# Two pairs of first maxima moved into the second layer's end, and three PSUM places made slices of one tile

## The chip, the core and the metric

The kernel runs on one core of a Trainium2 chip. TensorE (PE) multiplies matrices into PSUM, VectorE (DVE) and ScalarE (ACT) read PSUM and work elementwise, GpSimd (POOL) works in SBUF, SyncE (SP) issues most DMAs. The engines run their own instruction streams and wait for each other on semaphores. The metric is the device time of one execution in microseconds, median of the runs shown; lower is better.

## The reference, cut to what matters

The input is eight images of 32 x 32 positions with 256 channels. Three blocks follow each other: a hybrid of a 3x3 convolution (192 channels) and attention with relative position logits (8 heads of 8 channels), then plain attention with one head of 128, then a mixture of two of eight feed-forward experts.

```python
# layer 0, on the group-normalised image
conv_out = lax.conv_general_dilated(x, conv_w, ..., padding='SAME') + conv_b
logits = jnp.einsum('bnid,bnjd->bnij', qf, kf) + rel_w + rel_h
weights = jax.nn.softmax(logits, axis=-1)
attn = jnp.einsum('bnij,bnjd->bnid', weights, vf)
x = x + concatenate([conv_out, attn @ attn_w + attn_b], axis=3)
# layer 1, on the layer-normalised tokens t
w = softmax(Q @ K.T / sqrt(U)); t = t + (w @ V) @ W_o + b_o + norm(t)
# then the experts, on norm(t), chosen for each image by a router
```

## The kernel before, in words

The program goes through the eight images one after the other and keeps PE's instruction stream in the order in which the code is written (`manual_schedule` for PE). The other engines' streams in this part are ordered by the framework's scheduler. The framework puts in the semaphore waits, from the tiles that each instruction reads and writes. The expert layer comes after all images, as a part of its own (from L1025).

**The first layer's attention** (`conv_layer_attention`, L681) works on four *units* of an image, each 4 of 8 heads and 512 of 1024 queries. In `Unit.score` (L574) two matmuls (K=24, 512 columns) write a 128 x 1024 tile `lg` of logits, and DVE takes its maxima into `my` (L591). Sixteen of these, in eight pairs, give a unit its maxima. `Unit.fold` (L600) turns them (`pmx`), adds the row term and sends the result `mb` by three DMAs into row 32 of the operand `F`. Then `Unit.weigh` (L615) recomputes logits transposed, now with K=32, into `st` (128 x 512, one PSUM bank), and ACT writes their exponentials to `PT` (L631). `Unit.gather` (L633) multiplies `PT` with the values into `po`.

The loop at L694 counts steps `s`. A step scores one pair for unit `s // 8` and weighs one block of 128 keys for the unit ten steps back (`lead = NT + LAG = 10`). So three stretches come out: ten steps that only score (the **lead**), 22 that score and weigh, and ten that only weigh. In a step that does both, PE's order is score, weigh head 1, weigh head 3, gather half, score, weigh head 0, weigh head 2, gather half. In the steps that only weigh, heads 1 and 3 share one wide `lg` tile. Beside them stand the transposes and statistics of the next image (`norm_steps`, L295).

**The convolution** (`conv_steps`, L501) is 72 products an image, twelve to a tile `pc` (L515). ACT copies a full tile into `m` (L524, two buffers) and POOL adds it into the image `T` in up to four additions (L527 to L538). `Conv.run(n)` emits n products. They are spread as fillers: `more` and `fill` emit 36 of the next image's while the second layer starts, two stand in the second layer's end, and 34 fall in the lead, three to a step. Their tile comes from `place[0]`, which is `po_tile` during the fill and `st_tile` in the lead.

**The fill** (`attention_layer`, L758, and `input_steps`, L385): PE alternates the next image's projections (`pk`, `pvv`), its relative position products (`prel`, `tpw`), convolution products and the transposes of the normalised tokens (`tpn`, L779). POOL adds the tokens `n` (two buffers) into `T` at L780 and the bias `bo` at L784.

**The second layer's attention** (also `attention_layer`): eight blocks of rows. `scores(i)` writes `lg1`, DVE takes the row maximum, ACT the exponential; `turn(i)` transposes it through two `st` tiles, one copied out by DVE (L856) and one by ACT (L858); `gather(ib)` sums with the values into `po`; `project(ib)` multiplies with `W_o` into an `st` tile, which DVE adds into `T` (L880). Afterwards POOL sums `acc` for the router (L915, L917) and stores the image to `Td` (L922); `token_mean` (L925) finishes that sum, at step 5 of the next image.

**PSUM** has eight banks: `ps_lg` two tiles of two banks, `ps_st` three tiles of one, `ps_po` one. Everything but `lg`, `po`, `prel`, `tpw` and `tpx` goes through `st_tile`.

```python
def st_tile(name):
    return ps_st.tile([P, 512], FP, tag="st", name=name)      # bufs=3
```

Of the kernel before, what the change touches and what calls it, by code (L numbers as in the profile page):

```python
# [10 lines left out]
FP = mybir.dt.float32  # L11
I32 = mybir.dt.int32
AF = mybir.ActivationFunctionType
ALU = mybir.AluOpType
# [3 lines left out]
P = 128  # L18
# [18 lines left out]
def kernel(  # L37
# [54 lines left out]
    with ExitStack() as ph:  # L92
# [3 lines left out]


        ps_lg = ph.enter_context(tc.tile_pool(name="ps_lg", bufs=2, space=PSUM))
        ps_st = ph.enter_context(tc.tile_pool(name="ps_st", bufs=3, space=PSUM))
        ps_po = ph.enter_context(tc.tile_pool(name="ps_po", bufs=1, space=PSUM))  # L100


# [14 lines left out]
        def po_tile(name):  # L117
            return ps_po.tile([P, 512], FP, tag="po", name=name)

        def st_tile(name):  # L120
            return ps_st.tile([P, 512], FP, tag="st", name=name)


        raws = []
# [260 lines left out]
        def input_steps(b, held):  # L385
# [3 lines left out]
            xn = held["xn"].rearrange("p k a c j x -> p k (a c j x)")  # L389
            kq = work.tile([P, S], FP, tag="kq", name="kq")  # L390

            pv = st_tile("pvv").rearrange("p (j c) -> p j c", c=DK)
            for q in range(2):
                pk = st_tile("pk")
                for kc in range(KC):
# [30 lines left out]
            for g in range(NG):  # L426
# [12 lines left out]
                vb.rearrange("p (h d) -> p h d", d=DH).unsqueeze(1).to_broadcast([P, NT, NH, DH]),  # L439
                ALU.add,  # L440
            )
            yield 0.43, 2


# [10 lines left out]
            for which in range(2):  # L455
                for half in range(2):
                    prs = lg_tile("prel")
                    for i in range(16):
                        a = half * 16 + i
                        for g in range(NG):  # L460
                            rows = slice(DK + 32 * g, DK + 32 * g + 32)
                            dst = prs[:, g, i * 32 : (i + 1) * 32]
                            if which == 0:
                                table, mov, m = half_w, kqv[rows, :, a], WW - 1 - a
                            else:
                                table, mov, m = half_h, kqv[rows, a, :], HH - 1 - a
                            for k in range(2):
                                nc.tensor.matmul(
                                    dst[64 * k : 64 * k + 64], lhsT=table(rows, m, k), rhs=mov, start=True, stop=True
                                )  # L470
                        if i == 7:
                            yield 1.4, 4 - (which == half == 0)
                    for g in range(NG):
                        if which == 0:
                            dst = rw[g].rearrange("p (x y) -> p y x", y=WW)[:, half * 16 : half * 16 + 16, :]
                            src = prs[:, g, :].rearrange("p (y x) -> p y x", x=HH)
                        else:
                            dst, src = rh[g][:, half * 512 : (half + 1) * 512], prs[:, g, :]
                        if g == 0:
                            nc.vector.tensor_copy(dst, src)  # L480
                        else:
                            nc.scalar.copy(dst, src)
                    if which == 0 and half == 1:
                        for g in range(NG):
                            nc.sync.dma_start(out=rwd[g], in_=rw[g])
                    yield 1.4, 4 - (which == half == 0)

            for t4 in range(2):
                tp = lg_tile("tpw").rearrange("p q (t g c) -> p (q t) g c", t=2, g=NG)
# [51 lines left out]
        class Unit:  # L541
# [29 lines left out]
                self.pts = {}  # L571
                self.po = None

            def score(self, n, rwq):  # L574

                i, hl = divmod(n, HG)
                if hl == 0:
                    self.my = work.tile([P, WW, HG], FP, tag="my", name="my", bufs=2)
                my = self.my
                lg = lg_tile("lg")  # L580
                for a in range(2):
                    r = 32 * ((hl + 2 * a) % HG)
                    nc.tensor.matmul(  # L583
                        lg[:, a, :],
                        lhsT=self.F[r : r + 24, a, 0, i * P : (i + 1) * P],
                        rhs=KM[self.g][r : r + 24, a].rearrange("p e k -> p (e k)"),
                        start=True,
                        stop=True,
                    )

                nc.vector.tensor_reduce(  # L591
                    my[:, :, hl], lg.rearrange("p a (y x) -> p y a x", y=WW), AX.XY, ALU.max
                )
                if hl == HG - 1:
                    nc.vector.tensor_tensor(
                        my, my, rwq[:, self.half * 4 + i, self.g].rearrange("p (y h) -> p y h", h=HG), ALU.add
                    )
                    nc.vector.tensor_reduce(self.mx[:, i, :], my.rearrange("p y h -> p h y"), AX.X, ALU.max)
# [78 lines left out]

        NU = 2 * NG
        LAG = 2

        def conv_layer_attention(b, units, kq, rh, rwd, rwq, conv, early, ahead, more):  # L681

# [1 line left out]

            at = work.tile([P, NT, DK], FP, tag="at", name="at")
            units.append(Unit(1, kq, rh, rwd))
            left = conv.left
            lead = NT + LAG  # L690
            first = left % (3 * lead)
            conv.run(first)
            left -= first
            for s in range(NU * NT + lead + 2):  # L694
                u, j = divmod(s, NT)
                w, k = divmod(s - lead, NT)
                g, l = divmod(s - lead - 1, NT)
                score, weigh, gather = u < NU, 0 <= w < NU, 0 <= g < NU


                if score:
                    units[u].score(2 * j, rwq)
                    if weigh:
                        units[w].weigh(k, (1,), st_tile)
                        units[w].weigh(k, (3,), st_tile)
                    if gather and l:
                        units[g].gather(l, (0, 1))
                    units[u].score(2 * j + 1, rwq)
                    if weigh:
                        units[w].weigh(k, (0,), st_tile)  # L710
                        units[w].weigh(k, (2,), st_tile)
                    if gather:
                        units[g].gather(l, (2, 3) if l else (0, 1, 2, 3))
                else:
                    if weigh:
                        units[w].weigh(k, (0,), st_tile)
                        units[w].weigh(k, (2,), st_tile)
                        units[w].weigh(k, (1, 3), lg_tile)
                    if gather:
                        units[g].gather(l, (0, 1, 2, 3))  # L720
# [3 lines left out]
                    units[g - 1].settle(at)  # L724
                if g == NU:
                    more(NT // 2, 0)
                if not weigh:
                    todo = -(-left // (lead - s))
                    conv.run(todo)
                    left -= todo  # L730
                if s == 5:
                    early()
                if s > NU * NT:
                    next(ahead, None)
                if s % NT == 0 and 0 < u <= NU:
                    units[u - 1].fold(u - 1)
                if s % NT == 0 and 0 < u < NU - 1:
                    units.append(Unit(u + 1, kq, rh, rwd))
# [16 lines left out]
            more(0, 4)  # L755


        def attention_layer(b, fill, conv):  # L758

# [6 lines left out]
            fill(4.5)  # L768
            nT = pt_tile("nT").rearrange("p (k s) -> p k s", k=KC)
            for q in range(2):  # L770
                tps = [st_tile("tpn").rearrange("p (j t) -> p j t", j=4) for _ in range(KC)]
                for j in range(4):
                    t = q * 4 + j
                    n = work.tile([P, C], FP, tag="n", name="n", bufs=2)
# [6 lines left out]
                    fill(0.7)  # L781
                for kc in range(KC):
                    nc.scalar.copy(nT[:, kc, q * 512 : (q + 1) * 512], tps[kc].rearrange("p j t -> p (j t)"))
            nc.gpsimd.tensor_tensor(T[b], T[b], bo.to_broadcast([P, NT, C]), ALU.add)  # L784
            fill(1000.0)
            conv.whole()

# [58 lines left out]
            def turn(i):  # L846
                if i % NIB == 0:
                    pts[i // NIB] = pt_tile("pt").rearrange("p (j q) -> p j q", j=NT)
                for c in range(2):
# [2 lines left out]
                        jc = c * 4 + j  # L852
                        nc.tensor.transpose(tp[:, j, :], prs[:, i % 4, jc * P : (jc + 1) * P], ident)
                    dst = pts[i // NIB][:, c * 4 : c * 4 + 4, (i % NIB) * P : (i % NIB + 1) * P]
                    if c == 0:
                        nc.vector.tensor_copy(dst, tp)  # L856
                    else:
                        nc.scalar.copy(dst, tp)  # L858

            def gather(ib):  # L860
                po = po_tile("po1")
                pt = pts.pop(ib)
                for jc in range(NT):
                    nc.tensor.matmul(  # L864
# [19 lines left out]
            for i in range(NT):  # L884
                scores(i)
                if i < 2:
                    values(i)
                ib, odd = divmod(i - 3, NIB)
                if ib >= 0 and not odd:
                    os = gather(ib)  # L890
# [1 line left out]
                    turn(i - 1)  # L892
                if ib >= 0 and not odd and i + 1 < NT:
                    project(ib, os)
            turn(NT - 1)
            project(NT // NIB - 2, os)
            os = gather(NT // NIB - 1)
            conv.place[0] = st_tile
            conv.run(2)
            project(NT // NIB - 1, os)  # L900

# [53 lines left out]
        with tc.manual_schedule(engines={mybir.EngineType.PE, mybir.EngineType.DVE}):  # L955
# [12 lines left out]
                    next(other, None)  # L968
            for _ in other:
                pass  # L970
        with tc.manual_schedule(engines={mybir.EngineType.PE}):
            conv = Conv(0)
            means = []
            for b in range(B):
                last = b + 1 == B
                if not last:
                    T[b + 1] = load_image(b + 1)

                def early():
                    if means:  # L980
                        token_mean(*means.pop())

                def ahead():

                    yield from norm_steps(b + 1, held)

                now, held = held, {}
                conv.place[0] = st_tile
                steps = iter(()) if last else input_steps(b + 1, held)

                following = Conv(b + 1)
# [1 line left out]
                def more(n, products):  # L993
# [11 lines left out]
                    early,  # L1005
                    iter(()) if last else ahead(),
                    more,
                )
                conv = following

# [6 lines left out]
                        us -= took  # L1017
                        conv.run(products)

                means.append((b, *attention_layer(b, fill, conv)))  # L1020
                del T[b]
            token_mean(*means.pop())

# [282 lines left out]
```

## Time and profile before

The median of three runs is 2404.95 us (2403.57 to 2409.04). The profiled execution took 2407.99 us, with a span of 2406.2 us from its first to its last instruction, so 1.8 us lie outside the span.

| stretch of the profiled execution | us from the span's start | length, us | PE busy | granted clock |
|---|---|---|---|---|
| lead of the fifth image | 998.7 to 1031.6 | 32.9 | 31.9 | 0.90 |
| steps that score and weigh | 1031.6 to 1109.4 | 77.8 | 77.6 | 1.00 |
| steps that only weigh | 1109.4 to 1144.3 | 34.9 | 32.7 | 1.00 |
| fill | 1144.3 to 1181.2 | 36.9 | 36.5 | 1.00 |
| q and k of the second layer | 1181.2 to 1188.1 | 6.9 | 6.9 | 1.00 |
| the rest of the second layer | 1188.1 to 1232.3 | 44.2 | 44.2 | 1.00 |

Images follow each other every 231 to 234 us; the mean granted clock of the whole span is 0.974. Times of a stage are read off the starts of the first matmuls of each kind. A busy PE in a row is not PE at its peak, since a matmul's record also holds time in which it waits in PE's pipeline behind the one before it. In a row of the profile, "PE" is the matmul and "PEld" its weight load; one fp32 matmul of the code is two of each. "<-" after an idle time names what ended it.

### The profile page before, as it was taken

Reading aid. Unit: us, or ns where it says so; the run is one execution under the profiler, and the core shown is the slowest. Engines: PE = TensorE matmul, PEld = TensorE weight load, DVE = VectorE, ACT = ScalarE, POOL = GpSimd, SP = SyncE. Lnnn points to the kernel's source line nnn. Section 1 sums busy time; section 2 is a strip of 40 time slices with the busy share of each in tenths; the row PEclk is TensorE's granted clock in tenths of the full one; section 3 lists DMA queues with packets and bytes.
Section 4 is the critical chain, followed back from the end, with each engine's and each line's share of the span. In section 5 each row is a group of like instructions: output and inputs, shape, how many; then the busy total and the mean of one; then the engine's idle time right before and its main releaser. Section 6 shows DMA issues by size and latency. Waiting matters only on the chain. (4 is left out here: it accounts for less than half of the span.)

```text
span 2406.2 us, 41836 instructions
## 1 busy us (share of the span) xinstructions
PE 2317.1 (96%) x17273; PEld 1308.3 (54%) x17273; DVE 1481.2 (62%) x2653; ACT 1022.7 (43%) x1709; POOL 475.7 (20%) x446
## 2 busy tenths in 40 slices
PE   6999999999999999999999999999998789999998
PEld 5535743664366437633763376337533556666665
DVE  7676487558756874777477747774773524444443
ACT  2255436534543463256326632563255322222332
POOL 4201130312022102300230023002301032222231
PEclk7999999999999999999999999999998989999999
DMA  4520242234123403340324033403330122122210
GB/s 124 83 43 26 46 96 39 42 61 77 26 51 61 83 11 58 71 73 3 58 71 74 3 58 80 65 5 56 76 52 2 55 90 70 70 70 71 83 49 26
DMA packets 71468, 135.82 MB, mean 56 GB/s; under 512 B 12000, under 2 KB 24168, under 8 KB 69232
## 3 DMA queue, kind: packets, MB, share of 16 engines
q1 hardware_dynamic: 65488, 115.47, 24.1%
q0 software_dynamic: 3056, 15.73, 1.9%
q8 instruction: 136, 2.23, 0.4%
q10 hardware_dynamic: 2736, 1.97, 0.3%
q14 instruction: 52, 0.43, 0.1%
HBM read 53.43 MB, written 25.17 MB: 33 GB/s over the span
## 5 line engine op out<-in xcount | busy, mean ns | idle before, releaser
L591 DVE TENSOR_REDUCE my<-lg 128x32 f32<-128x1024 f32 x512 | 617.9, 1223 | 170.4 <-PE st L623 125.9
L631 ACT ACTIVATE PT<-st 128x512 f32<-128x512 f32 (+1 forms) x944 | 541.6, 633 | 306.3 <-PE st L623 302.3
L623 PE MATMUL st<-F,km 32*128 32x512 f32 x2048 | 545.3, 641 | 16.6 <-DMA F<-mb 11.2
L583 PE MATMUL lg<-km,F 24*128 24x512 f32 x2048 | 538.8, 650 | 8.0 <-DVE my L591 4.8
L640 PE MATMUL po<-PT,vall 128*32 128x256 f32 (+1 forms) x3200 | 315.1, 453 | 2.9 <-ACT PT L631 2.4
L583 PEld LDWEIGHTS lg<-km,F 24*128 24x128 f32 x2048 | 156.8, 188 | 188.7 <-issue 111.0
L515 PE MATMUL pc<-convw,gdif 128*128 128x192 f32 x1152 | 240.3, 351 | 1.0 <-ACT convw L280 0.7
L640 PEld LDWEIGHTS po<-PT,vall 128*32 128x32 f32 x3200 | 67.1, 108 | 314.5 <-issue 280.0
L515 PEld LDWEIGHTS pc<-convw,gdif 128*128 128x128 f32 x1152 | 192.5, 197 | 72.4 <-issue 65.2
L623 PEld LDWEIGHTS st<-F,km 32*128 32x128 f32 x2048 | 177.6, 184 | 95.5 <-issue 43.5
L1236 PE MATMUL py<-w,hT 128*128 128x256 f32 x1024 | 223.6, 379 | 0.0
L1219 PE MATMUL phd<-n2T,w 128*128 128x512 f32 x512 | 223.4, 594 | 0.0
L1236 PEld LDWEIGHTS py<-w,hT 128*128 128x128 f32 x1024 | 194.7, 190 | 33.2 <-issue 7.7
L311 POOL TENSOR_TENSOR T<-T,l0b 128x2048 f32<-128x2048 f32 x8 | 36.4, 4544 | 633.9 <-PE tpx L304 633.9
L1219 PEld LDWEIGHTS phd<-n2T,w 128*128 128x128 f32 x512 | 96.8, 191 | 114.7 <-issue 107.6
L1243 DVE TENSOR_TENSOR r<-py,n 128x256 f32<-128x256 f32 x64 | 27.1, 423 | 213.1 <-PE py L1236 213.1
L1226 ACT ACTIVATE hT<-phd,b1c 128x512 f32<-128x512 f32 x128 | 86.3, 686 | 96.3 <-PE phd L1219 96.1
L524 ACT COPY m<-pc 128x384 f32<-128x384 f32 x48 | 23.7, 493 | 238.9 <-PE pc L515 217.5
L833 PE MATMUL lg<-qkv 128*128 128x512 f32 x256 | 121.1, 595 | 0.0
L780 POOL TENSOR_TENSOR T<-T,n 128x256 f32<-128x256 f32 x64 | 47.3, 747 | 372.8 <-DVE n L775 372.8
L842 DVE TENSOR_REDUCE nm<-lg 128x1 f32<-128x1024 f32 x64 | 78.1, 1220 | 67.5 <-PE lg L833 67.5
L864 PE MATMUL po<-pt,qkv 128*128 128x256 f32 x512 | 115.7, 379 | 0.0
(250 smaller groups left out, 2625.8 us busy)
## 6 DMA issues: line engine op xcount, KB each, us to landing
F<-rh SPq DMA_DIRECT2D x256, 128.0 KB
F<-kq SPq DMA_DIRECT2D x256, 64.0 KB
F<-rwd SPq DMA_DIRECT2D x256, 64.0 KB
w<-in_L_ffn_W_dram SPq DMA_DIRECT2D x32, 512.0 KB
rwd<-rw SPq DMA_DIRECT2D x16, 512.0 KB
Td<-T POOLq DMA_DIRECT2D x8, 1024.0 KB, 8.0
T<-Td SPq DMA_DIRECT2D x8, 1024.0 KB
out_dram<-yo SPq DMA_DIRECT2D x16, 512.0 KB
```

The costliest lines, as they stand in the source:

```text
L515: nc.tensor.matmul(pc[:, v, :], lhsT=gflat[:, 2 * pair + v, kc, at : at + P], rhs=convw[:, 2 * pair + v, dy, kc * CO : (kc + 1) * CO], sta ...
L583: nc.tensor.matmul(lg[:, a, :], lhsT=self.F[r : r + 24, a, 0, i * P : (i + 1) * P], rhs=KM[self.g][r : r + 24, a].rearrange("p e k -> p (e ...
L591: nc.vector.tensor_reduce(my[:, :, hl], lg.rearrange("p a (y x) -> p y a x", y=WW), AX.XY, ALU.max)
L623: nc.tensor.matmul(st[:, i, :] if len(heads) > 1 else st, lhsT=KM[self.g][r : r + 32, a, e, :], rhs=self.F[r : r + 32, a, e, :], start=Tru ...
L631: nc.scalar.activation(self.pts[j][:, hs, :], st, AF.Exp)
L640: nc.tensor.matmul(self.po[32 * hl : 32 * hl + 32, cols], lhsT=vall[:, j, h * (DH + 1) : h * (DH + 1) + 32], rhs=self.pts[j][:, hl, cols], ...
L833: nc.tensor.matmul(lg[:, h, :], lhsT=qk[0][:, i * P : (i + 1) * P], rhs=qk[1][:, h * 512 : (h + 1) * 512], start=True, stop=True,)
L842: nc.vector.tensor_reduce(nm, lg, AX.X, ALU.max, negate=True)
L864: nc.tensor.matmul(po[:, 0:IB], lhsT=v1[:, jc, :], rhs=pt[:, jc, :], start=jc == 0, stop=jc == NT - 1)
L1219: nc.tensor.matmul(phd, lhsT=ws[k][0][:, kc, f * P : (f + 1) * P], rhs=n2T[:, kc, q * 512 : (q + 1) * 512], start=kc == 0, stop=kc == KC - 1,)
L1226: nc.scalar.activation(hT[:, k * NF + f, :], phd, AF.Gelu, bias=b1c[:, f, k * B + b : k * B + b + 1])
L1236: nc.tensor.matmul(py, lhsT=hT[:, k * NF + f, j * P : (j + 1) * P], rhs=ws[k][1][:, f, :], start=k == 0 and f == 0, stop=k == TOPK - 1 and ...
```

## The change

- The three tiles of `ps_st` become one tile `st3` of three banks. `st_tile` hands out its slices in turn; a slice can be kept (for `pvv` and the two `tpn` tiles) and is then skipped. `two_tile` hands out the first two slices together as a third wide place for logits.
- Two of the ten pairs that the lead scores, `maxima(0)` and `maxima(1)`, are emitted inside the end of the second layer of the image before. For all but the first image the lead starts at step 2.
- In the lead every third score goes to `two_tile` (`APART`); the others to `lg_tile`.
- 48 of the 72 products now stand in the second layer's end and the lead, six to a step; 24 stay in the fill, two or three to a step. Their tile is always `po_tile`.
- POOL's stream in this part is in the order of the code too. The image load and `token_mean` move to the lead's last step, and the addition of `bo` into the second layer.
- The last `turn` copies both halves on ACT; the last `gather` uses an `st` slice.

```diff
-        ps_st = ph.enter_context(tc.tile_pool(name="ps_st", bufs=3, space=PSUM))
+        ps_st = ph.enter_context(tc.tile_pool(name="ps_st", bufs=1, space=PSUM))
...
-        def st_tile(name):
-            return ps_st.tile([P, 512], FP, tag="st", name=name)
+        st3 = ps_st.tile([P, 3, 512], FP, tag="st", name="st")
+        turn_of = [0]
+        kept = {}
+        def st_tile(name, keep=False):
+            while True:
+                turn_of[0] = (turn_of[0] + 1) % 3
+                if turn_of[0] not in kept.values():
+                    break
+            if keep:
+                kept[name] = turn_of[0]
+            return st3[:, turn_of[0], :]
+        def two_tile(name):
+            assert not kept
+            turn_of[0] = 1
+            return st3[:, 0:2, :]
...
-                            yield 1.4, 4 - (which == half == 0)
+                            yield 1.4, 2
...
-                    yield 1.4, 4 - (which == half == 0)
+                    yield 1.4, 2 + which
...
-            def score(self, n, rwq):
+            def score(self, n, rwq, tile):
...
-                lg = lg_tile("lg")
+                lg = tile("lg")
...
+        def pair(units, s, rwq):
+            u, j = divmod(s, NT)
+            for n in (2 * j, 2 * j + 1):
+                units[u].score(n, rwq, two_tile if s * 2 + n % 2 in APART else lg_tile)
+        APART = range(5, 2 * (NT + LAG), 3)
...
-            for s in range(NU * NT + lead + 2):
+            if not done:
+                conv.run(n_tile)
+            plan = [0] * done + share(conv.left, lead - done)
+            for s in range(done, NU * NT + lead + 2):
...
-                if score:
-                    units[u].score(2 * j, rwq)
+                if score and not weigh:
+                    pair(units, s, rwq)
+                elif score:
+                    units[u].score(2 * j, rwq, lg_tile)
...
-                if s == 5:
+                if s == NT:
+                    conv.run(plan[s] // 2)
+                    units[0].fold(0)
+                    conv.run(plan[s] - plan[s] // 2)
+                elif s < lead:
+                    conv.run(plan[s])
+                if s == lead - 1:
                     early()
...
-            nc.gpsimd.tensor_tensor(T[b], T[b], bo.to_broadcast([P, NT, C]), ALU.add)
             fill(1000.0)
...
-                    if c == 0:
+                    if c == 0 and i + 1 < NT:
...
+                if i == 1:
+                    nc.gpsimd.tensor_tensor(T[b], T[b], bo.to_broadcast([P, NT, C]), ALU.add)
...
+            maxima(0)
             turn(NT - 1)
             project(NT // NIB - 2, os)
-            os = gather(NT // NIB - 1)
-            conv.place[0] = st_tile
+            maxima(1)
+            os = gather(NT // NIB - 1, st_tile)
             conv.run(2)
             project(NT // NIB - 1, os)
...
-        with tc.manual_schedule(engines={mybir.EngineType.PE}):
+        with tc.manual_schedule(engines={mybir.EngineType.PE, mybir.EngineType.Pool}):
...
-                if not last:
-                    T[b + 1] = load_image(b + 1)
-
                 def early():
                     if means:
                         token_mean(*means.pop())
+                    if not last:
+                        T[b + 1] = load_image(b + 1)
```

## The prediction

> **What bounds the kernel now.** I read the page first, then the busy time by stage of the fifth image, then the timeline inside two of its stages.
>
> ```profile
> PE 2317.1 (96%) x17273; PEld 1308.3 (54%) x17273; DVE 1481.2 (62%) x2653; ACT 1022.7 (43%) x1709; POOL 475.7 (20%) x446
> L631 ACT ACTIVATE PT<-st 128x512 f32<-128x512 f32 (+1 forms) x944 | 541.6, 633 | 306.3 <-PE st L623 302.3
> L623 PE MATMUL st<-F,km 32*128 32x512 f32 x2048 | 545.3, 641 | 16.6 <-DMA F<-mb 11.2
> ```
>
> PE is busy nearly everywhere. ACT waits 302 us for `st`, PE hardly ever for ACT: three places of `st` keep PE ahead.
>
> ```profile
> core 0: us, PE busy (x) PEld busy (x) DVE busy (x) ACT busy (x) POOL busy (x), PEclk, DMA share, GB/s
> 998.70:1031.60 32.90, 31.94 (x151) 17.28 (x150) 28.08 (x40) 2.16 (x6) 20.07 (x25) 0.90 0.45 106
> 1031.60:1109.40 77.80, 77.62 (x640) 27.25 (x640) 60.96 (x74) 47.11 (x86) 0.99 (x1) 1.00 0.34 58
> 1109.40:1144.30 34.90, 32.69 (x239) 10.47 (x236) 25.50 (x60) 27.44 (x41) 4.55 (x1) 1.00 0.01 3
> 1144.30:1181.20 36.90, 36.53 (x687) 31.80 (x685) 16.70 (x44) 11.93 (x21) 15.12 (x17) 1.00 0.35 68
> 1181.20:1188.10 6.90, 6.90 (x18) 3.09 (x17) 2.61 (x3) 1.73 (x4) 2.41 (x2) 1.00 0.60 80
> 1188.10:1232.30 44.20, 44.20 (x225) 33.33 (x223) 22.89 (x50) 18.53 (x32) 0.00 (x0) 1.00 0.18 28
> ```
>
> The rows are the lead, the 22 steps that score and weigh, the 10 that only weigh, the fill, q and k, and layer 2. Only the lead has much that is not PE's own work: DVE holds it, and its clock is 0.90. The others are packed with matmuls.
>
> ```profile
> 1041.14 0.91 PE L623 MATMUL st<-F,km 32*128 32x512 f32 x2
> 1041.66 0.59 PE L583 MATMUL lg<-km,F 24*128 24x512 f32 x2
> 1041.67 0.80 PE L623 MATMUL st<-F,km 32*128 32x512 f32 x2
> ...
> 1042.34 1.08 ACT L631 ACTIVATE PT<-st 128x512 f32<-128x512 f32 x2 [0.56 <-PE st L623]
> 1042.40 0.64 PE L640 MATMUL po<-PT,vall 128*32 128x256 f32 x8
> 1042.97 0.70 PE L583 MATMUL lg<-km,F 24*128 24x512 f32 x2
> 1042.99 0.70 PE L623 MATMUL st<-F,km 32*128 32x512 f32 x2
> ```
>
> One half step: a score and two `st` matmuls run side by side on four row groups (each fp32 matmul is two passes), all in 1.07 us, then `po` in 0.57. The next half step starts while ACT still works on the last `st`.
>
> ```profile
> 1023.72 2.09 PE L583 MATMUL lg<-km,F 24*128 24x512 f32 x8
> 1025.87 2.36 DVE L591 TENSOR_REDUCE my<-lg 128x32 f32<-128x1024 f32 x2 [1.43 <-PE lg L583]
> ```
>
> The same matmul while the granted clock is 0.5 (1022.7 to 1029.5): 2.07 us from weight load to the end of the second pass, against 1.12 at full clock.
>
> **The change: what it means to do.** A convolution product costs 0.351 us (8 matmuls in 1.40), two scores 1.07. Before, the lead holds 34 x 0.351 + 10 x 1.07 + 1.2 (pmx, pmt) = 23.8 us of PE work and lasts 32.0 to 34.4 (33.4 over seven images). After, 46 x 0.351 + 8 x 1.07 + 1.2 = 25.9, with a DVE need of about 2.6 a step against PE's 3.2. Two pairs go into the end of layer 2, which is packed: +2.1. Twelve products leave the fill, packed too: -4.2. Pool's fixed order puts a tile's four adds (3.2 us) ahead of one `T+=n`, whose `n` buffer a later tpn needs: +0.8. Together about -7 an image, -50 in all.
>
> The queues carry it. Unit 0's loads were issued by 1190, long before the moved pairs; unit 1's take SP 18 us (1225 to 1243) and step 8 comes some 20 us into the lead. The image load that moves to the lead's end is needed 70 us later. Pool's 4.6 us `T+=bo` has the whole of layer 2's start, and its 13 us of `acc` end before the third convolution tile needs `m` back. The convolution's single `po` place is copied out (0.49) behind a pair of scores (1.07). If that cover went, it would cost 0.6 a tile.
>
> **The change: what it adds unsaid.** The three places become slices of one tile. In the built program's waits every matmul that writes one slice waits for the reader of the slice *before* it, not for that of three before: a `st` waits for the exponential of the `st` just ahead of it. In the built program of before, the wait named the exponential three tiles back. So the three places work as one. Queued behind the waiting matmul are all of PE's: the next `st`, `po`, the next score.
>
> The Trainium skill's PSUM page (PSUM: the matmul accumulator, PSUM bank collisions) asks for a guard by bank and quadrant, under which three places in three banks owe each other nothing, and the time would be the -50 above; no run here shows it.
>
> *Steps that score and weigh.* From one `st` to the next: matmul 1.12, to ACT 0.08, exponential 0.60, back to PE 0.05: 1.85 us. Four a step: 7.4, with `po` and score inside the waits, against 77.8 / 22 = 3.5 now.
>
> That is at full clock, which I do not expect to last. I weighted the trace's matmul records by the part of the 128x128 array that they fill. In the 3.4 us ahead of each fall of the clock that weight was at most 0.35 (0.28, 0.29, 0.35, 0.29, 0.30, 0.34, 0.29 for the seven from 538 to 1705), though PE counted as busy; stretches of 0.37 or more never led to a fall. At half clock it stayed after 0.66 to 0.71 and came back after 0.77 or more. A serial step fills 4 x 0.854 x 32/128 + 4 x 0.854 x 24/128 + 0.85 = 2.35 us in 7.4: 0.32. So the clock falls within a step or two, and at half it is 4.7 in 11.7, 0.40: it does not return in this stage.
>
> The skill's page TensorE: Matmul & The Clock Gate (HAM oscillation) blames only idle gaps over about 3.4 us; the lead's falls, with gaps under 1.5, differ from it, and by it the time would be that of the first rival. Its next section (A second HAM failure mode) has micro-idle PSUM cycling swing the clock to and fro, which would land between.
>
> At half clock: 2.07 + 0.08 + 0.60 + 0.05 = 2.80 to the second `st`; `po` (about 1.0) and the next score's issue stretch the other link to 3.04. A step is 11.7, 22 steps 257. Two folds and two settles also take a place, 1.9 each with DVE's read; the first us at full clock give 2 back: 263, so **+185**.
>
> *Steps that only weigh*: 10. Two `st` in series, then `po`: 6.7 at half clock, 3.95 at full. Score 1,3 has its own place, and with `po` fills a stretch that may bring the clock back: I take 6.0, and 10 for fold, settle, the two group means and transposes: 70, **+35** (13 to 43).
>
> *Fill*: from the first pk to the products the waits for kq (1.8), at (1.0), aT (1.5) and kq again (1.0) add 5.4; -4.2, +0.8, half clock left over 2: **+4**. *q and k*: three waits of 0.98 and one of 1.1: **+4**. *Layer 2*: each of eight transposing steps waits for its first half's copy: 0.95, or 1.75 where DVE's row maximum stands ahead; the first 2.6; three projections 0.72; delayed maxima 1.0. That is 15, and the moved pairs 2: **+17**. *Lead*: 29 (25.9, 1.0 where the second wide place waits for project's adds, 2 for the fold behind a maximum and the first `st`): **-4**.
>
> Sum +241 an image; six images 1446. The first has less lead to save, +244; the last no moved pairs, +227. 1917 on the profiled execution's 2408 is 4325; the median of three was 3 below its profile, so about 4320.
>
> **Rivals.** (1) The same waits at full clock: 22 x 7.4 + 6 = 169 (+91), weighing +12, fill +2, rest as above: +122 an image, about 3370. For it: 0.32 is near 0.35. Against: one low stretch of 3.4 us is enough, and every stretch here is low. (2) The clock comes and goes: 3400 to 4080; for it, the weigh-only steps might free it, but the scoring steps would have to as well. (3) Faster: the three slices do not hold each other up on the chip, so everything under "unsaid" is nothing and the 7 us an image are kept, 2355. For it: the slices do not overlap. Against: the waits stand in the program. It decides if the exponential of one place runs while PE writes the next. (4) No change: the serial waits hide beside `po` and scores; they cannot, since those are 3.3 us of a step and the chain 7.4.
>
> **Numbers.** Half clock through the scoring stage 0.77 (4080 to 4560 by the weighing steps' bounds and 15 us an image elsewhere), to and fro 0.08, full clock 0.10, faster 0.04, within 0.2% 0.01; 0.2% is about what a measurement of this kernel can tell from no change. The range reaches into the second rival: 3850 to 4560.
>
> **What would show it.** PEclk near 0.5 over the scoring stages; `st` idle before its weight load on ACT PT, over 0.5 us each; ACT's exponentials one by one, 2.8 us apart; the lead at about 29 us and full clock; the FFN's last 490 us unchanged. Wrong if `st` matmuls start while ACT reads their neighbour, or if the step stays at 3.5 us.

## The result, and the profile after

The changed kernel takes 4468.82 us (median of four runs, 4452.36 to 4471.28) against 2404.26 for the kernel before: a ratio of 1.8565, 95% interval 1.8514 to 1.8616. The profiled execution spans 4450.6 us at a mean granted clock of 0.678. The forecast was 4320 with a range of 3850 to 4560.

First the page of the changed kernel: the engines' busy time, the clock over forty slices of the span, and the groups that were shown of before.

```profile
PE 3872.6 (87%) x17273; PEld 1693.2 (38%) x17273; DVE 1474.6 (33%) x2645; ACT 1077.2 (24%) x1717; POOL 474.5 (11%) x446
...
PEclk7556865568556955577556955686556855589999
...
L641 PE MATMUL st<-F,km 32*128 32x512 f32 x2048 | 1707.2, 1074 | 332.8 <-ACT PT L649 321.9
L649 ACT ACTIVATE PT<-st 128x512 f32<-128x512 f32 (+1 forms) x944 | 589.1, 633 | 1971.2 <-PE st L641 1902.1
```

The same 17273 matmuls are there. The `st` matmul's mean went from 641 to 1074 ns, and PE, which had waited 16.6 us ahead of all of them, now waits 322 us for ACT's exponentials. An exponential still takes 633 ns, but ACT now waits 1902 us for `st` instead of 302: the two engines take turns. The clock is at half speed for most of every image (355 of the fifth one's 491 us), and back at 0.97 in the FFN at the end, the last slices.

The busy time by stage of the fifth image, from the end of the image before: lead, scoring and weighing, weighing alone, fill, q and k, layer 2. The columns are those of the same view in the prediction.

```profile
2026.10:2055.80 29.70, 28.25 (x172) 18.88 (x171) 24.75 (x38) 4.02 (x9) 21.02 (x26) 1.00 0.44 87
2055.80:2312.70 256.90, 225.55 (x668) 57.66 (x666) 62.37 (x73) 52.93 (x89) 0.93 (x2) 0.52 0.11 21
2312.70:2384.70 72.00, 60.95 (x207) 15.18 (x207) 24.45 (x64) 27.02 (x38) 4.53 (x1) 0.62 0.01 1
2384.70:2446.20 61.50, 54.23 (x661) 44.94 (x661) 15.82 (x38) 12.32 (x20) 10.68 (x15) 0.61 0.28 49
2446.20:2456.40 10.20, 7.82 (x17) 2.94 (x18) 1.38 (x2) 0.59 (x1) 5.87 (x3) 1.00 0.45 50
2456.40:2517.60 61.20, 49.37 (x231) 33.08 (x229) 26.28 (x51) 18.74 (x33) 0.00 (x0) 0.97 0.07 14
```

Cut in the same way, before has 35.4, 80.0, 31.4, 36.9, 6.9 and 42.9. (The table ahead of the prediction cuts the first three a little differently: 32.9, 77.8 and 34.9.) The scoring stage alone is 177 us longer, at a clock of 0.52. From the timeline of one half step in it (start, duration; in brackets the idle time before and what ended it):

```profile
2100.58 1.06 PE L601 MATMUL lg<-km,F 24*128 24x512 f32 x2
2100.60 1.06 PE L641 MATMUL st<-F,km 32*128 32x512 f32 x1
...
2101.74 0.60 ACT L649 ACTIVATE PT<-st 128x512 f32<-128x512 f32 x1 [2.48 <-PE st L641]
...
2102.39 2.07 PE L641 MATMUL st<-F,km 32*128 32x512 f32 x2 [0.73 <-ACT PT L649]
...
2104.38 1.08 PE L658 MATMUL po<-PT,vall 128*32 128x256 f32 x8
2104.49 0.60 ACT L649 ACTIVATE PT<-st 128x512 f32<-128x512 f32 x1 [2.16 <-PE st L641]
2105.39 1.22 PE L601 MATMUL lg<-km,F 24*128 24x512 f32 x2
```

Before, two `st` and a score ran side by side and the next pair began while ACT read the last. Here the second `st` starts 0.05 us after the exponential of the first has ended (2101.74 + 0.60 = 2102.34), takes 2.07, and its own exponential starts at 2104.49, 2.75 after the first one's. Each exponential stands alone.

### The profile page after: what moved, and what is told of

Same layout as the page of the kernel before. It is cut to its first block, busy times and chain, and to the rows that moved or that the text cites. A ratio compares the mean times of both kernels' runs of the same rounds, so it can differ in the third digit from the quotient of the medians.

```text
span 4450.6 us, 41925 instructions
## 1 busy us (share of the span) xinstructions
PE 3872.6 (87%) x17273; PEld 1693.2 (38%) x17273; DVE 1474.6 (33%) x2645; ACT 1077.2 (24%) x1717; POOL 474.5 (11%) x446
## 3 DMA queue, kind: packets, MB, share of 16 engines
q1 hardware_dynamic: 65488, 115.47, 13.3%
## 5 line engine op out<-in xcount | busy, mean ns | idle before, releaser
L641 PE MATMUL st<-F,km 32*128 32x512 f32 x2048 | 1707.2, 1074 | 332.8 <-ACT PT L649 321.9
L649 ACT ACTIVATE PT<-st 128x512 f32<-128x512 f32 (+1 forms) x944 | 589.1, 633 | 1971.2 <-PE st L641 1902.1
L601 PE MATMUL lg<-km,F 24*128 24x512 f32 x1888 | 866.7, 985 | 2.2 <-DMA F<-kq 2.2
L641 PEld LDWEIGHTS st<-F,km 32*128 32x128 f32 x2048 | 411.2, 290 | 1081.8 <-ACT PT L649 1047.4
L658 PE MATMUL po<-PT,vall 128*32 128x256 f32 (+1 forms) x3200 | 512.6, 736 | 0.0
L601 PEld LDWEIGHTS lg<-km,F 24*128 24x128 f32 x1888 | 223.3, 271 | 295.4 <-issue 286.5
L533 PE MATMUL pc<-convw,gdif 128*128 128x192 f32 x1152 | 285.3, 400 | 0.7 <-ACT convw L297 0.7
L892 PE MATMUL st<-ident,pr 128*128 128x128 f32 x512 | 83.6, 287 | 79.1 <-DVE nm L882 35.7
L883 ACT ACTIVATE pr<-lg,nm 128x1024 f32<-128x1024 f32 x64 | 71.3, 1114 | 197.2 <-DVE nm L882 197.2
L892 PEld LDWEIGHTS st<-ident,pr 128*128 128x128 f32 x512 | 58.9, 144 | 117.4 <-DVE pt L895 38.5
```

The lines of the kernel that those rows point to most:

```text
L533: nc.tensor.matmul(pc[:, v, :], lhsT=gflat[:, 2 * pair + v, kc, at : at + P], rhs=convw[:, 2 * pair + v, dy, kc * CO : (kc + 1) * CO], sta ...
L601: nc.tensor.matmul(lg[:, a, :], lhsT=self.F[r : r + 24, a, 0, i * P : (i + 1) * P], rhs=KM[self.g][r : r + 24, a].rearrange("p e k -> p (e ...
L641: nc.tensor.matmul(st[:, i, :] if len(heads) > 1 else st, lhsT=KM[self.g][r : r + 32, a, e, :], rhs=self.F[r : r + 32, a, e, :], start=Tru ...
L649: nc.scalar.activation(self.pts[j][:, hs, :], st, AF.Exp)
L658: nc.tensor.matmul(self.po[32 * hl : 32 * hl + 32, cols], lhsT=vall[:, j, h * (DH + 1) : h * (DH + 1) + 32], rhs=self.pts[j][:, hl, cols], ...
```

## The experiments

Times of runs with an interval are medians of several; the others are of one run. "Stage" is the one that scores and weighs, in the fifth image; the stage before takes 80.0 us, in the changed kernel 256.9.

**Three tiles instead of three slices.**

```diff
-        st3 = ps_st.tile([P, 3, 512], FP, tag="st", name="st")
+        st3 = [ps_st.tile([P, 512], FP, tag=f"st{k}", name=f"st{k}") for k in range(3)]
...
-            return st3[:, turn_of[0], :]
+            return st3[turn_of[0]]
...
-            return st3[:, 0:2, :]
+        two_tile = lg_tile
```

> The changed kernel with its three one-bank places of st as three tiles of their own instead of slices of one, taken in the same turn; the third wide place goes (its scores take the two old ones), and the moved pairs, the 48 products and Pool's order stay. If the slices wait for each other and that is what costs, about 2365 us (2340 to 2405): scoring stage back to 80 us at full clock, exponentials again ahead of one another. If the moved work itself (pairs in layer 2, products, Pool's order) cost the time, it stays above 4000 us.

Measured 2389.12 us, 0.9928 of before (0.9911 to 0.9944). The stage is 80.3 us at full clock. With all that was moved still in its new place, and only the third wide place missing, the slowdown is gone. It is the slices; the moved work was even worth something, though 24 us less than I expected.

**Slices alone, nothing moved.** The kernel before with the first of these edits the other way round; a place that is kept is skipped, as in the changed kernel.

```diff
-        ps_st = ph.enter_context(tc.tile_pool(name="ps_st", bufs=3, space=PSUM))
+        ps_st = ph.enter_context(tc.tile_pool(name="ps_st", bufs=1, space=PSUM))
...
-            return ps_st.tile([P, 512], FP, tag="st", name=name)
+        st3 = ps_st.tile([P, 3, 512], FP, tag="st", name="st")
...
+            return st3[:, turn_of[0], :]
```

> The kernel before with one edit: its three st places become slices of one tile, in the same turn; nothing is moved and there is no third wide place. If the slices alone are the cause: about 4530 us (4430 to 4620), above the changed kernel by its longer lead (5 us an image) and by twelve more products in a fill at half clock. If the moved work is the cause, or both are needed: near 2405 us.

Measured 4493.78 us, and the stage 257.8 us at a clock of 0.51. One edit that changes no instruction (the page counts the same ones on every engine), only to which tile a place belongs, costs 87% over the 2406.23 us of before beside it. The two runs together settle the cause.

**Two places back instead of one.**

```diff
-        st3 = ps_st.tile([P, 3, 512], FP, tag="st", name="st")
+        st2 = ps_st.tile([P, 2, 512], FP, tag="st", name="st")
+        st1 = ps_st.tile([P, 512], FP, tag="st1", name="st1")
...
+                k = (0, 2, 1, 2)[turn_of[0]]
...
+            return st1 if k == 2 else st2[:, k, :]
```

> The changed kernel with its third wide place as a tile of two banks and the third st place as a tile of its own, used in the turn first slice, single, second slice, single: a st then waits for the exponential of two before, not of the one before, and the wide place is kept. If the time goes by how many places back the wait reaches: two st in 1.85 us at full clock, so 3.7 us a step at least against 3.5 with three, the array 0.5 to 0.6 filled, clock full: 2430 to 2650 us. If sharing a tile at all costs the half clock: above 4000.

Measured 2588.67 us. Two slices still share a tile, but in this turn the wait reaches two places back; the windows of the stage:

```profile
1130.60:1221.90 91.30, 91.30 (x672) 34.68 (x668) 62.19 (x75) 48.88 (x89) 1.33 (x2) 1.00 0.32 60
```

That is 4.15 us a step (91.3 / 22, folds included), 11 us an image over three tiles, at full clock. So it is the distance of the wait that counts, not the sharing as such. The rest of this kernel's distance from three tiles lies outside the stage, most of it in the fill (47.6 us at a mean clock of 0.82, against 40.4 at 0.83) and, by some 3 us each, in weighing alone and layer 2. Here the third wide place is kept, and the lead is 27.2 us against 28.2 with three tiles: that place is worth 1 us an image.

**Why the clock is at half.** The next four runs add to each of the 22 steps four useless matmuls (`filler`) into the place of the next score, which overwrites them: two in PE's waits for the exponential, two ahead of the scores. Only their shape differs: R rows, C columns of the array, N columns of data.

```diff
+        def filler(lg):
...
+            nc.tensor.matmul(lg[0:C, 0, 0:N], lhsT=ident[0:R, 0:C],
+                rhs=convw.rearrange("p v d c -> p (v d c)")[0:R, 0:N], start=True, stop=True)
```

Wide, R = C = 128 and N = 512:

> The changed kernel with four useless fp32 matmuls of 128x128x512 (0.85 us each at full clock) added to each of the 22 steps that score and weigh, two of them in PE's waits for the exponential, into the place of the next score, which overwrites them. If the half clock comes from the thin filling of the array: the filling rises from 0.32 to about 0.6, the clock stays full in that stage, a step takes 8.6 us instead of 11.6, and the kernel gets faster by about 530 us in spite of 700 more dense matmuls: 3935 us (3800 to 4100). If the clock plays no part beside the waits: slower than the changed kernel, above 4470.

Measured 3993.0 us. The windows of the stage, wide:

```profile
1832.40:2040.20 207.80, 207.52 (x843) 59.25 (x842) 62.39 (x74) 52.88 (x89) 0.89 (x2) 1.00 0.15 26
```

Narrow, R = C = 32 and N = 512:

> As the run with the wide fillers, the same number, length and places, but each filler uses 32 rows and 32 columns of the array, a sixteenth. If the clock goes by the filled share of the array: the share stays under 0.36, the clock falls as before and a step takes 13.7 to 17 us: 4840 to 5430 us. If the clock goes by PE's busy time or its gaps: full clock as with the wide fillers, 3800 to 4100 us.

Measured 5339.31 us; the stage, narrow:

```profile
2509.50:2880.50 371.00, 371.00 (x843) 67.92 (x842) 62.38 (x73) 52.82 (x89) 0.82 (x2) 0.51 0.08 14
```

The same 696 extra matmuls make the changed kernel 476 us faster if they are wide and 871 slower if they are narrow. PE is busy throughout in both, so neither busy time nor gaps set this clock. Both runs were forecast by the filled share of the array. But these two change rows and columns together, so the next one keeps the rows.

Tall, R = 128, C = 32, N = 512:

> As the runs with the wide and the narrow fillers, each filler now 128 rows by 32 columns: all rows of the array at work, a quarter of it filled. If the clock goes by the product of rows and columns: the mean filling of the stage falls from 0.60 (wide, measured) to about 0.30, the clock is half and a step takes about as long as with the narrow ones (16.9 us): 5200 to 5450 us. If it goes by the rows at work alone: full clock as with the wide fillers, near 3993 us.

```profile
1813.10:2010.00 196.90, 196.63 (x843) 48.16 (x842) 62.38 (x73) 52.83 (x89) 0.82 (x2) 1.00 0.15 27
```

Measured 3949.68 us at full clock: my expectation was wrong, and so was the measure behind it. A matmul of 128 rows and 32 columns keeps the clock up as one of 128 columns does. I then weighed the matmul records of the traces again, in the windows of 3.41 us that the clock's changes mark (within a trace all changes lie whole multiples of 3.41 us apart), by rows at work (added up over matmuls that run side by side, at most all 128) instead of rows times columns. The table has the means over the stage, the lowest window in brackets. A record counts only for the time that its data need in the array (0.427 us for 512 columns at full clock, half of the prediction's 0.854), not for the weight load, so the busy share is below that of the windows.

| kernel | PE busy by these records | rows x columns | rows | clock |
|---|---|---|---|---|
| changed | 0.75 | 0.40 (0.17) | 0.40 (0.17) | 0.52 |
| wide | 0.81 | 0.60 (0.50) | 0.61 (0.50) | 1.00 |
| narrow | 0.89 | 0.30 (0.13) | 0.37 (0.22) | 0.51 |
| tall | 0.85 | 0.36 (0.30) | 0.64 (0.52) | 1.00 |
| short (below) | 0.77 | 0.35 (0.24) | 0.52 (0.37) | 1.00 |

Over whole traces, the first 40 us left out: of 7486 windows at full clock in the twelve traces that the clock survived, 8 are at or below the highest one of their own trace that it did not, by rows; 491 by rows times columns (468 of them in the tall and the short run); over 1000 by busy time. By rows, every fall comes after a window of at most 0.39, and no window that the clock survived is below 0.37. The way back is less sharp: the clock returned after windows of 0.68 to 1.0, and sometimes stayed low after up to 0.80, so the 0.77 that the prediction read from one trace is no sharp limit. These figures depend on where in a record the data's time is put: with it at the records' ends, falls come after windows of up to 0.43, and 188 surviving windows lie at or below such a one by rows, 1036 by rows times columns. The order of the measures stays, the limits hold to a few hundredths.

Short, R = 128, C = 32, N = 256, so that the fillers in the waits fit into them:

> As the run with the tall fillers (128 rows by 32 columns; 3949.7 us, stage of scoring and weighing 196.9 us an image, 8.95 us a step, full clock), each filler half as long (256 columns of data, 0.43 us), so that those in the waits fit into them. If the clock goes by rows at work: (2.35 + 4 x 0.43) / 7.8 = 0.52 of the rows, above the 0.38 under which it falls, full clock; a step then shows the bare chain of waits at full clock, 7.4 us by the prediction, and 0.4 of filler that is not hidden: 7.4 to 8.0, the stage 163 to 176, the kernel 3950 - 8 x (21 to 34) = 3680 to 3780 us. If the tall fillers kept the clock by their length and not by their rows: half clock again, above 4470 us.

```profile
1710.40:1883.50 173.10, 165.13 (x842) 50.23 (x838) 62.42 (x73) 52.93 (x89) 0.94 (x2) 1.00 0.18 31
```

Measured 3755.37 us: half the filler, the same full clock, now forecast by rows. A step is 173.1 / 22 = 7.87 us, folds and unhidden filler included. That splits the stage's 177 us: at most 93 for the waits at full clock (173.1 - 80.0), at least 84 for the clock (256.9 - 173.1).

**Why the fill stays slow.** Four wide matmuls in a row ahead of the first `tpn` of the changed kernel:

```diff
+            burst = lg_tile("lg")
+            for _ in range(4):
+                nc.tensor.matmul(burst[:, 0, :], lhsT=ident, rhs=..., start=True, stop=True)
             nT = pt_tile("nT").rearrange("p (k s) -> p k s", k=KC)
```

> The changed kernel with four useless matmuls of 128x128x512 in a row (6.8 us at half clock) inside the fill, ahead of the first tpn. In the changed kernel the fill lasts 61.5 us, 47.8 of them at half clock, though it is nearly packed. If it stays slow only because no stretch of it fills 0.75 of the array: the burst brings the clock back, the work behind it takes half as long, and in spite of the burst the fill shrinks by about 10 us: near 4400 us (4360 to 4440). If the half clock has another reason there: the burst is paid in full, about 4520 us.

Measured 4416.1 us, 36 below the lowest run of the changed kernel. In the first seven images the fill, with the burst in it, is 55.0 to 56.3 us (mean 55.9), 20.7 to 23.9 of them at half clock; in the changed kernel it is 51.6 to 61.6 (mean 59.6), 20.7 to 47.8 at half. In five of the seven the clock was at half when the burst began, as in the second image:

```profile
953.75 4.53 PE L810 MATMUL lg<-convw,ident 128*128 128x512 f32 x8
958.42 1.25 PE L486 MATMUL prel<-kq,bdw 32*64 32x32 f32 x64
```

The burst starts at half clock, and from 955.6 the clock is full; the `prel` behind it takes 1.25 us, where the one ahead of it took 1.93. In all five the clock came back 1.6 to 1.9 us after the burst's start, so the burst cost 4.4 to 4.6 us and not 6.8, and half clock lasted 23.9 us, against 45.0 to 47.8 in six of the changed kernel's seven fills. In the other two images, the third and the fifth, the clock had come back before the burst, which took 3.6 us there; the changed kernel's third fill (51.6 us) also came back early, without one. So a fill gained 3.7 us in the mean, burst included, and not the 10 that I expected, and some 10 of the 36 us lie outside the fills. Still, in five images useless work on the busiest engine made the fill shorter: it lacked one dense window. A burst of thin matmuls in the same place was not run.

**What the intended part is worth.** With three tiles the fill has 34.2 us in three images, and 40.5 in four, 13.7 of them at half clock. The timelines of Pool, DVE and PE ahead of one such fall (at 925.3):

```profile
914.25 0.83 POOL L815 TENSOR_TENSOR T<-T,n 128x256 f32<-128x256 f32 x1 [31.18 <-DVE n L810]
919.38 0.60 POOL L544 TENSOR_TENSOR sd<-m 128x192 f32<-128x192 f32 x1 [4.29 <-ACT m L538]
...
921.56 1.01 POOL L552 TENSOR_TENSOR T<-T,sd 128x384 f32<-128x384 f32 x1
922.52 1.41 POOL L815 TENSOR_TENSOR T<-T,n 128x256 f32<-128x256 f32 x2
```

```profile
923.28 1.12 DVE L810 TENSOR_SCALAR n<-T,lmv 128x256 f32<-128x256 f32 x2 [2.05 <-POOL T L815]
```

```profile
924.13 0.44 PE L814 MATMUL st<-ident,n 128*128 128x128 f32 x2 [1.03 <-DVE n L810]
```

In Pool's fixed order a convolution tile's four adds stand ahead of the second `T+=n`. Pool stands still for 4.29 us, waiting for their `m`, though that `n` has been ready for 2.1 us (since 917.24, by DVE's timeline); then the adds take 3.2; only then does the buffer of `n` come free. PE waits 1.03 us, beside `prel` matmuls of 32 rows; the window ahead of the fall has 0.38 of the rows at work. Whether the clock falls depends on where the window lies. The wait is the same, 1.03 us, in all seven images; in the four where the clock fell, a window ends 0.1 to 1.2 us after it, in the other three 2.6 to 3.1. Two runs undo this, in different ways. Pool left to the scheduler:

```diff
-        with tc.manual_schedule(engines={mybir.EngineType.PE, mybir.EngineType.Pool}):
+        with tc.manual_schedule(engines={mybir.EngineType.PE}):
```

> The run with three tiles of their own (2389 us), with Pool's order left to the scheduler again. There the fill lasts 34.2 us in three images and 40.5 in four, with 13.7 us of half clock, after tpn has waited some 1 us for n, whose buffer Pool frees only behind a convolution tile's four adds. If Pool's fixed order is the cause: n comes in time, the fill is 33 to 34 us in all images without half clock: 2389 - 4 x 6.3 - 7 = about 2357 us (2345 to 2370). If Pool's order plays no part: 2389 again, or later by what the scheduler does to the image load.

Measured 2393.03 us, 0.9939 of before (0.9919 to 0.9958): a miss. The fill did become 33 us in every image, as expected, but q and k take 13.3 us instead of 7.0, 6.8 of them at half clock. Pool, ACT and PE there:

```profile
938.84 4.54 POOL L924 TENSOR_TENSOR T<-T,bo 128x2048 f32<-128x2048 f32 x1
```

```profile
944.50 0.36 ACT L547 ACTIVATE sd<-sd 128x192 f32<-128x192 f32 x1 [4.25 <-POOL sd L545]
...
946.09 1.06 ACT L818 COPY nT<-st 128x512 f32<-128x512 f32 x2
```

```profile
946.72 8.37 PE L830 MATMUL st<-nT,wqkv 128*128 128x512 f32 x12 [3.15 <-ACT nT L818]
```

The scheduler puts the 4.5 us of `T+=bo` ahead of the second tile's adds; ACT waits 4.25 us for Pool's `sd`, and the copies of `nT` that q needs are queued behind that. In this kernel `T+=bo` is written in layer 2, but without the fixed order Pool does not keep it there. So holding it back, which the prediction had counted at nothing, is worth some 6 us an image here. The other way keeps Pool's order and moves only the adds (with ACT's scaling of `sd` among them) behind the next `T+=n`:

```diff
                     nc.gpsimd.tensor_tensor(T[b][:, t, :], T[b][:, t, :], n, ALU.add)
+                    while late:
+                        late.pop(0)()
+                    hold[0] = t < NT - 1
                     fill(0.7)
...
+                                (late.append if hold[0] else lambda f: f())(adds)
```

> The run with three tiles of their own (2389 us), Pool's order still fixed, but in the fill a convolution tile's four adds stand behind the next T+=n instead of ahead of it; nothing else is moved. If that one place in Pool's order holds n up: as with Pool left free, 2345 to 2370 us, no half clock in the fill. If something else in Pool's order does (the adds of bo, the image load): 2385 to 2392.

Measured 2358.08 us, 0.9796 of before (0.9778 to 0.9815), the fastest version here. Its fifth image:

```profile
978.00:1006.20 28.20, 27.99 (x167) 19.26 (x166) 24.61 (x35) 3.11 (x8) 20.13 (x25) 1.00 0.44 87
1006.20:1086.50 80.30, 80.30 (x673) 27.91 (x672) 62.23 (x77) 48.96 (x90) 1.68 (x2) 1.00 0.37 68
1086.50:1118.00 31.50, 29.36 (x206) 9.30 (x205) 23.09 (x59) 25.35 (x37) 4.54 (x1) 1.00 0.02 3
1118.00:1150.90 32.90, 32.56 (x664) 27.91 (x662) 16.67 (x44) 10.21 (x18) 9.38 (x13) 1.00 0.32 69
1150.90:1158.20 7.30, 7.09 (x18) 2.95 (x17) 2.61 (x3) 3.11 (x6) 6.59 (x4) 1.00 0.65 89
1158.20:1204.00 45.80, 45.80 (x233) 32.82 (x231) 26.16 (x51) 18.87 (x33) 0.61 (x1) 1.00 0.21 32
```

Full clock in every row, no wait of `tpn` for `n` in the first seven images that is over 0.3 us, and 226.0 us an image against 233.5.

## Why the prediction was right, and where it was not

**Slices wait for each other.** Right. The wait that was read in the built program is the one in the timeline, and the second run shows that it suffices. The rule weighed in the prediction, from the Trainium skill's page PSUM — Partial Sum Buffer (PSUM bank collisions raise a hardware error), would let three places in three banks owe each other nothing; the run with three tiles agrees, 80.3 us for the stage, but the built program does not use that freedom for slices of one tile.

**Scoring stage, +185.** Measured 177, 256.9 us where 263 was forecast. The two links were 2.80 and 3.04; the timeline has 2.75 and 3.07 between exponentials (2101.74, 2104.49, 2107.56). 22 steps of these are 256.1, so the folds and settles, for which the sum had 6 more, cost next to nothing. At full clock the first rival put the stage at 169; the short filler's 173.1, with some filler unhidden, is in keeping with it.

**The clock stays at half there.** Right, by a measure that was half wrong. The prediction weighed by the part of the array; the tall filler shows that columns do not count. It did no harm here, since the `st` and score matmuls have all 128 columns and the four `po` beside each other fill them, so both measures give a serial step 0.32 at full clock and 0.40 at half, which is the mean measured. Nor did the clock come and go: it was at half for 249.0 of the stage's 256.9 us. The Trainium skill warns of idle gaps of PE over some 3.4 us (TensorE: Matmul & The Clock Gate, HAM oscillation). Such gaps are not what brings the clock down here: the stage with narrow fillers is PE-busy for all of its 371.0 us and at 0.51.

**Weighing alone, +35.** Measured 40.6 (31.4 to 72.0), inside 13 to 43. With the stage before it, where the cut between the two plays no part, 217.5 against 220.

**Fill, +4.** Wrong: +24.6. This is the term that was mis-sized, and within it the "half clock left over 2". In the fifth image nothing was left over: the clock is full when the fill begins (2384.6). It falls inside the fill, at 2391.3 and again at 2401.6, after waits that the prediction had listed as time alone (PE waits 1.64 us for `kq`, at 2388.2 and again at 2400.2), and the second time it stays down:

```profile
2401.60:2442.50 40.90, 40.90 (x600) 36.78 (x599) 11.88 (x32) 6.96 (x11) 7.77 (x11) 0.50 0.35 63
```

Half clock held for 47.8 of the 61.5 us, which is worth 23.9 if PE sets the pace; the rest of the fill, 61.5 - 23.9 = 37.6, is within 1 us of before. The prediction had noted that the clock comes back only after a window of 0.77 and did not ask whether the fill has one. With `prel` matmuls of 32 rows between the products, the windows of this stretch have 0.59 to 0.71 of the rows at work, above where the clock falls, and it came back only after one of 0.86. The burst supplied such a window, and the fill shrank. The seven fills are 11 to 21 us each over the forecast, 131 in all; the profiled execution, 4452.36 us, is 127 over its forecast of 4325.

**Q and k, +4; layer 2, +17; lead, -4.** Measured +3.3, +18.3 and -5.7 (-3.5 against an image whose lead before had no half clock).

**An image, +241.** Measured 258.0 in the fifth (233.5 to 491.5) and 1541 for the six against 1446; the first and the last 261 and 242 against 244 and 227. The FFN and what follows is 495.9 us against 496.1, unchanged as expected. The bounds 4080 and 4560 of the half-clock case lie 240 us to both sides of the sum; the parts named for them, -22 to +8 in the weighing steps and 15 elsewhere, come to some 4020 and 4500 over eight images. The measured median lies inside both.

**The intended part, -7 an image and 2355 without the waits (third rival's price).** The version with the adds moved, which lacks the third wide place, gives -7.5 and 2358: lead -7.2, fill -4.0, layer 2 +2.9, q and k +0.4, the rest +0.4. My four terms (-7.5, +2.1, -4.2, +0.8) add up to -8.8 and were carried as 7, which the text did not explain. The term for Pool's order, +0.8, was the wrong one: in the change as it stands it costs 1.3 us in every fill with three tiles, and 6.3 more wherever the clock falls with it, 31 us over the kernel (2389.12 - 2358.08).

## What to carry to other kernels

Before a buffer is cut into slices of one tile, look at what the scheduler waits for: if it tracks tiles and not slices, several places become one, and no instruction has to change for a kernel to take 1.9 times as long. A stall on TensorE can then be paid twice, as it was here: once as the wait (at most 93 us of the stage's 177) and once as the half clock (at least 84). A stage that is only moderately dense, as the fill was, can keep the half clock long after the stall. With an order fixed by hand, a waiting instruction holds up everything emitted behind it, so put the work whose input is ready, and whose buffer another engine needs, ahead of it.

## What was unexpected in the hardware

As far as these runs show, the granted clock follows the rows of the array at work, not TensorE's busy time and not the columns: by the reckoning above it was halved only after 3.41 us windows with at most 0.39 of the rows at work, and given back only after 0.68 or more. Only 32 and 128 rows were tried in fillers. Adding 696 useless matmuls of 128 rows and 32 columns, 256 columns of data each, made a slow kernel 713 us faster (4468.82 to 3755.37), and the same number with 32 rows, twice as long, made it 871 slower.
